# A bank of their own for the transposed chunks of P, three banks for the scores, earlier loads of the network and a new order at the end

## The chip, the cores and the metric

The kernel runs on one core of one Trainium2 chip. The metric is the device time of one execution in microseconds (us). Three runs of the kernel before took 769.55, 768.00 and 767.49 us; their median is 768.0. One further execution was taken with the hardware profiler: 767.24 us, with a span of 765.5 us from the first to the last recorded instruction.

A core has a matrix engine (TensorE, PE in the profile; PEld is its loading of weights), three engines for elementwise work (VectorE or DVE, ScalarE or ACT, GpSimd or POOL) and a queue that issues transfers (SyncE or SP). Each engine works through its own list of instructions in order, and waits at semaphores for the others. TensorE writes its results to PSUM, which has eight banks of 128 x 512 float32; a bank can be given to the next product once its contents have been read out.

## The reference

One transformer layer on `x` (2 x 512 x 512, float32):

```python
q = (hidden_states @ Wq)   # 32 heads of 128
k = (hidden_states @ Wk)   # 8 heads of 128, each for 4 heads of q
v = (hidden_states @ Wv)
scores = jnp.einsum('bhqd,bhkd->bhqk', q, k) * scale   # causal mask, softmax
out = jnp.einsum('bhqk,bhkd->bhqd', probs, v)          # then @ Wo
x = _layernorm(x + attention)
# network: base product and bias, plus eight low-rank experts (rank 16),
# weighted by a sparsemax over eight logits
x = _layernorm(x + base_out + expert_out)
```

## The kernel before, in words

**Precision.** Every operand is split into a high and a low half in float16. A product is three matmuls, high by high, high by low and low by high (`mm3`, L228 to L231). All matmuls of projections, scores, P times V and output therefore have the line L231, and are told apart by their tiles.

**Groups and units.** The work of attention is 16 groups (g, b): a head of K and V with its four heads of Q, for one of two batches. The order of the groups is in L739. A group has four units i = 0 to 3. A unit has 128 rows of scores for each of four steps j (four heads times 32 queries), over n = 128 i + 32 (j + 1) keys. For each unit the kernel has these pieces:

- `proj` (L350): the next group's projections. Unit 0 carries K and the first head of Q, unit 1 the second head, unit 2 V, unit 3 the last two heads. Each is 12 matmuls of 512 columns (tiles pk, pq, pvp) in a bank of tag "pj", evacuated by ScalarE (L235) and VectorE (L236).
- `unit_a` (L362): four scores s, each three matmuls. VectorE masks and takes the row's extreme (L420), ScalarE takes the exponential in place in PSUM (L425), and in pairs `cut_p` forms the reciprocal (L376, L378), the high half (ScalarE, L388) and the low half (VectorE, L391) of P in SBUF, tile phl. Only then is the score's bank free.
- `unit_t` (L438): P is transposed in chunks of up to eight blocks of 128 x 128 on TensorE (`turn_blocks`, L342, tile px). Chunks are copied to SBUF (tile pt) alternately by ScalarE (L345) and VectorE (L348).
- `unit_b` (L450): P times V, tile pv, in the bank "PV", evacuated to o.
- `unit_c` (L491): the output product, 12 matmuls of 512 columns, tile pw, in the bank "wo"; VectorE adds it to the accumulator acc (L504).

**PSUM.** The eight banks are two of tag "pj", four of tag "S" (scores), one "PV" and one "wo". The chunks px share the two "pj" banks with the projections.

**The order.** Within a step of the body, the scores of unit s stand beside the chunks and P times V of unit s - 1, the output product of unit s - 2 and the next group's projections. The order on each engine is made by a list scheduler from the pieces, its own costs and the room in SBUF and PSUM: an instruction whose bank is not yet free in its reckoning comes later in the list. The start (L784 to L875) and the end (`tail`, L930, with the tokens of `TAIL`, L923) are written by hand. In a token the letter is the piece and the digit the block of 128 rows (0 to 7; the last group has 4 to 7): n and N are the layernorm of attention's output, a, p and q the scores and the two cuts of the last group's units, t and b, o their chunks and P times V, c, d their output product, capital letters T, B, O, C, D the same for the group before, X, l, r, s, h, m, e the network's steps, f and F its layernorm and store.

**Preparation.** `plan` and `at` (L881 to L911) attach the loading, measuring and splitting of later weights to units: a generator is advanced at the units that are named. `behind_all` (L887) issues a step no earlier than given instructions. `ffn_setup` (L509) prepares the network: four loads of the base weights (braw), two of the expert's first factor (lraw), one of the second (lorab), one of the bias, then sums of squares on ScalarE (L527) after an addition to the diagonal on GpSimd (L531), scales, and splits. In the kernel before, braw takes the room "base1", and lraw and lorab take three of the six rooms of tag "raw" in which the attention's weights land. `late_x(1, ...)` is the second conversion of x for batch 1.

Of the kernel before, what the change touches and what calls it, by code (L numbers as in the profile page):

```python
# [8 lines left out]
F32 = mybir.dt.float32  # L9
F32R = mybir.dt.float32r  # L10
F16 = mybir.dt.float16
# [6 lines left out]
P = 128  # L18
# [22 lines left out]
def kernel(  # L41
# [58 lines left out]
    def sync_load(dst, src):  # L100
        return nc.sync.dma_start(dst, src)
# [23 lines left out]

    def total(sq, n, name, tag="pj"):

        tot = ps.tile([P, 8], F32, tag=tag, name=f"tot{name}", bufs=4 if tag == "S" else 2)
        nc.tensor.matmul(tot[:, :n], ones, sq[:, :n], start=True, stop=True)
        return tot  # L130

# [96 lines left out]
    def mm3(dst, pairs, first=True, last=True):  # L228
        n = len(pairs)
        for j, (a, b) in enumerate(pairs):  # L230
            nc.tensor.matmul(dst, a, b, start=first and j == 0, stop=last and j == n - 1)  # L231

    def cut_psum(hi, lo, psrc, by):

        nc.scalar.activation(hi, psrc, AF.Copy, scale=by)  # L235
# [32 lines left out]
        LM[(g, b)] = lm  # L268

    def pj(name, tag="pj"):  # L270
        return ps.tile([P, S], F32, tag=tag, name=name, bufs={"pj": 2, "S": 4}.get(tag, 1))

    def mul_k(g, b, tag="pj"):
        pk = pj(f"pk{g}_{b}", tag)
# [62 lines left out]
    def turn_blocks(dst, src, tag="pj"):  # L337

        n = dst.shape[1]
        px = ps.tile([P, 8, P], F16, tag=tag, name="px", bufs=4 if tag == "S" else 2)  # L340
        for k in range(n):
            nc.tensor.transpose(px[:, k, :], src[:, k * P : (k + 1) * P], ident16)  # L342
        count.append(n)
        if len(count) % 2:
            nc.scalar.copy(dst, px[:, :n, :])  # L345
        else:

            nc.vector.tensor_scalar(dst.bitcast(I32), px[:, :n, :].bitcast(I32), 0, None, ALU.bitwise_or)  # L348
# [13 lines left out]
    def unit_a(g, b, i, whole=True):  # L362
# [52 lines left out]
        for j in range(4):  # L415
            n = full + (j + 1) * R
            qh, ql = (q2[:, a, HPG * i + j].rearrange("p h q -> p (h q)") for a in range(2))
            sc = ps.tile([P, S], F32, tag="S", name=f"s{g}_{b}_{i}_{j}", bufs=4)
            mm3(sc[:, :n], [(qh, k2[:, 0, :n]), (qh, k2[:, 1, :n]), (ql, k2[:, 0, :n])])
            nc.vector.tensor_tensor_reduce(  # L420
                out=sc[:, :n], in0=sc[:, :n], in1=mask[:, S - n :], scale=lm[:, 0:1], scalar=BIG,
                op0=ALU.add, op1=ALU.min, accum_out=st[:, 0, j : j + 1],
            )

            nc.scalar.activation(  # L425
                sc[:, :n], sc[:, :n], AF.Exp, bias=st[:, 0, j : j + 1], scale=-1.0, accum_out=st[:, 1, j : j + 1]
            )
            es.append(sc)
            if whole and j % 2:
                cut_p(j - 1)  # L430
# [4 lines left out]
                cut_p(h)  # L435
                yield

    def unit_t(g, b, i, tag="pj"):  # L438

        phl = PH.pop((g, b, i))  # L440
        nb = 8 * i + 6
        PT[(g, b, i)] = pt = sb.tile([P, nb, P], F16, tag="PT", name=f"pt{g}_{b}_{i}", bufs=2)
        for k in range(0, nb, 8):
            n = min(nb, k + 8)
            turn_blocks(pt[:, k:n, :], phl[:, k * P : n * P], tag)
            yield
# [3 lines left out]
    def unit_b(g, b, i):  # L450
# [27 lines left out]
        mm3(dst[:, 2:], pairs)  # L478
        yield
        o2 = sb.tile([P, 2, HPG, 4, R], F16, tag="O", name=f"o{g}_{b}_{i}", bufs=2)  # L480
        cut_psum(o2[:, 0], o2[:, 1], pv, 2.0**-15)
        OT[(g, b, i)] = o2
        yield

# [24 lines left out]
    def ffn_setup():  # L509


        raw = sb.tile([P, KC, HID], F32, tag="base1", name="braw")
        for c in range(KC):
            sync_load(raw[:, c, :], w_base[:, c, :])
        half = KC // 2
        lars = [sb.tile([P, 512], F32, tag="raw", name=f"lraw{k}", bufs=6)[:, : half * NL] for k in range(2)]
        for k, lar in enumerate(lars):
            sync_load(lar.rearrange("p (c n) -> p c n", c=half), lar_in[:, k * half : (k + 1) * half, :])
        lraw = load_raw(lora_b, "lorab")
        bias = sb.tile([P, HID + NE], F32, tag="ffnbias", name="ffnbias")  # L520
        sync_load(bias, bias_in.broadcast_to([P, HID + NE]))
        sq = sb.tile([P, KC, 4], F32, tag="fsq", name="fsq")
# [101 lines left out]
    def turn(t, urgent=False):  # L624
        a = acc[t]
        X[t] = x2 = sb.tile([P, 2 * KC, P], F16, tag="raw", name=f"x2{t}", bufs=6)
        px = ps.tile([P, KC, P], F32, tag="S" if urgent else "pj", name=f"px{t}", bufs=4 if urgent else 2)
        for c in range(KC):
            nc.tensor.transpose(px[:, c, :], a[:, c * P : (c + 1) * P], ident)
        H[t] = px  # L630
        nc.scalar.copy(x2[:, :KC, :], px)
# [13 lines left out]
        mm3(PA[t], pairs, last=False)  # L645

    def lora_in(t, last):
        tag, bufs = ("S", 4) if last else ("pj", 2)
# [28 lines left out]
        H[t] = hw  # L677

    def lora_mid(t, last):
        tag, bufs = ("S", 4) if last else ("pj", 2) if t == NT - 1 else ("wo", 1)  # L680
# [99 lines left out]
    def w_squares(dst, raw, tag):  # L780
        junk = pj("junk", tag)
        nc.scalar.activation(junk, raw, AF.Square, accum_out=dst)

    with tc.manual_schedule(engines={ET.PE, ET.DVE, ET.Activation, ET.Pool, ET.SP}):  # L784
# [40 lines left out]
        w_max(5)  # L825
        amax(mx[:, 6:7], mx[:, 9:13])
        for j in range(4):
            w_squares(sq0[:, j : j + 1], w_raw[j], "S")
        nc.scalar.activation(sq0[:, 4:7], mx[:, 4:7], AF.Square)
        w_lo(5, nc.vector)  # L830
        tot = total(sq0, 7, "0", "S")
# [15 lines left out]
            x_lo(1, c, nc.gpsimd)  # L847
        park(3, "S")
        for k in range(2):
            w_squares(mx[:, 17 + k : 18 + k], wo_raw[k], "S")  # L850
        for c in range(KC):
            x_max(1, c)
        amax(mx[:, 7:8], mx[:, 13:17])
        end_q(0, 0, 2, PK[2])
        end_v(0, 0, PK[5])
        for k in (2, 3):
            w_squares(mx[:, 17 + k : 18 + k], wo_raw[k], "S")
# [42 lines left out]
    at(prepare(0, ROWS, wo_raw), 0, 0, 0)  # L900
    at(prepare(1, JS, w1_raw), 1, 1, 1, 1, 2, 2, 2, 3, 3)
    at(prepare(1, ROWS), 4, 5, 5, 5, 6, 6, 7, 7)
    at(late_x(1, (1, 3)), 5, 6, 7, 7)
    at(ffn_setup(), 20, 21, 21, 21, 21, 21, 28, 28, 29, 29, 36)
    for g in range(1, NG):
        u = NT * (starts[g] - 2) - (3 if g == NG - 2 else 0)
        if g > 1:
# [13 lines left out]


    TAIL = """  # L923
    n3 a7 T7 C6 T7 N3 T7 D6 T7 B7 p7 q7 O7 X3 l3 a6 t7 C7 t7 r3 s3 t7 D7 t7 p6 q6 b7 h3 t6 o7 t6
    m3 t6 a5 c7 b6 p5 q5 e3 d7 t5 o6 n7 t5 a4 c6 N7 p4 q4 b5 f3 X7 t4 l7 m7 o5 r7 d6 n6 s7 c5 N6
    d5 h7 X6 n5 l6 b4 e7 o4 f7 r6 c4 N5 F7 s6 F3 X5 l5 d4 n4 m6 h6 r5 m5 s5 N4 e6 f6 h5 X4 l4 F6
    e5 r4 s4 f5 m4 h4 F5 e4 f4 F4
    """

    def tail():  # L930
# [116 lines left out]
```

## Time and profile before

| what | value |
|---|---|
| median of three runs | 768.0 us |
| profiled execution | 767.24 us |
| its span | 765.5 us |
| TensorE busy | 734.4 us |
| VectorE busy | 570.5 us |
| ScalarE busy | 443.7 us |
| GpSimd busy | 314.0 us |
| DMA, mean share of 16 engines, 100 to 650 us | 0.10 |
| granted clock, mean | 0.99 |

The profile is read by engine first. "Busy" counts the time of recorded instructions. The table of waits names the instruction that waited and the one that released it, with total, number and longest in us. A timeline row gives start and length in us, engine, line, operation, tiles, and in brackets the idle time before it with its releaser. A window row gives its bounds and length, then the busy time and number of instructions on TensorE, weight loads, VectorE, ScalarE and GpSimd, then the granted clock as a share of full speed, the DMA share and GB/s.

### The profile page before, as it was taken

How to read it: one execution, taken by the hardware profiler on the slowest of the kernel's cores; microseconds unless marked ns; L12 is line 12 of the kernel's file. 1: busy time of each engine (PE TensorE's matmuls, PEld its weight loads, DVE VectorE, ACT ScalarE, POOL GpSimd, SP SyncE). 2: the span in 40 equal slices, each digit the busy share in tenths (PEclk: the TensorE clock that was granted, in tenths of full speed). 3: DMA queues.
4: the chain of work that ended last, by engine and by line, in shares of the span. 5: the costliest groups of instructions: out<-in, count | busy, mean ns of one | idle time of the engine just before them, and what ended most of it. 6: DMA issues, size and time to landing. Idle time of an engine off the chain costs nothing.

```text
span 765.5 us, 15512 instructions
## 1 busy us (share of the span) xinstructions
PE 734.4 (96%) x5630; PEld 464.9 (61%) x5630; DVE 570.5 (75%) x1782; ACT 443.7 (58%) x1213; POOL 314.0 (41%) x500
## 2 busy tenths in 40 slices
PE   9899999999998999999999999999999999998896
PEld 6665666566664755666575655666575665655553
DVE  6885877769585777859686796959686687866787
ACT  6795564657466465746556475646556565345520
POOL 5779350726137198544209067243615020200011
PEclk9899999999999999999999999999999999999999
DMA  8540210110102011020202022020000000000001
GB/s 326 211 138 28 57 56 2 48 37 17 41 3 69 2 43 56 28 57 2 55 2 83 1 56 83 2 56 2 1 1 3 1 1 1 15 15 15 1 15 57
DMA packets 17357, 32.21 MB, mean 42 GB/s; under 512 B 1920, under 2 KB 2176, under 8 KB 17280
## 3 DMA queue, kind: packets, MB, share of 16 engines
q1 hardware_dynamic: 17280, 31.22, 13.0%
q8 instruction: 44, 0.72, 0.4%
q14 instruction: 33, 0.27, 0.1%
HBM read 29.12 MB, written 2.10 MB: 41 GB/s over the span
## 4 chain that ended last, share of the span: by engine, by line
PE 54%; DVE 16%; ACT 16%; issue 3%; POOL 2%; DMA 0%; POOLq 0%; ACTq 0%; DVEq 0%
PE pq L231 14%; PE pw L231 12%; PE pv L231 10%; PE s L231 7%; ACT phl L388 6%; ACT s L425 5%; PE px L342 5%; PE pvp L231 3%; DVE phl L391 3%; ACT pt L345 3%; DVE s L420 2%; DVE pt L348 2%; DVE mx L124 2%; PE pa L231 2%; DVE o L236 1%
## 5 line engine op out<-in xcount | busy, mean ns | idle before, releaser
L231 PE MATMUL pw<-w,o 128*128 128x512 f16 x768 | 185.3, 381 | 0.0
L231 PE MATMUL pq<-xT,w 128*128 128x512 f16 x672 | 154.1, 379 | 8.4 <-DVE pt L348 5.2
L391 DVE SCALAR_TENSOR_TENSOR phl<-s,ast,phl 128x128 f16<-128x128 f32 (+7 forms) x352 | 125.7, 418 | 32.8 <-ACT phl L388 30.9
L425 ACT ACTIVATE s<-s,ast 128x320 f32<-128x320 f32 (+15 forms) x256 | 118.5, 464 | 45.8 <-DVE ast L420 32.5
L420 DVE CUSTOM_DVE_ANT_0 s<-s,mask,lm 128x320 f32<-128x320 f32 (+15 forms) x256 | 118.0, 503 | 35.3 <-PE s L231 27.8
L231 PEld LDWEIGHTS <-w 128*128 128x128 f16 x840 | 80.5, 98 | 102.2 <-issue 16.6
L327 POOL TENSOR_SCALAR vt<-vt 64x512 f16<-64x512 f16 (+1 forms) x96 | 58.4, 610 | 164.1 <-ACT vt L235 158.4
L388 ACT ACTIVATE phl<-s,ast 128x96 f16<-128x96 f32 (+11 forms) x304 | 117.5, 478 | 14.1 <-DVE ast L378 13.0
L231 PEld LDWEIGHTS <-o 128*128 128x128 f16 x768 | 72.5, 100 | 69.8 <-issue 1.4
L231 PE MATMUL s<-k,q 128*128 128x480 f16 (+15 forms) x768 | 105.4, 281 | 6.3 <-ACT q L235 3.3
L231 PE MATMUL pv<-pt,vt 128*128 128x256 f16 (+1 forms) x960 | 107.9, 262 | 1.6 <-ACT pt L345 1.5
L231 PEld LDWEIGHTS <-vt 128*128 128x128 f16 x960 | 86.3, 98 | 23.6 <-issue 3.7
L342 PEld LDWEIGHTS <-phl 128*128 128x128 f16 x1152 | 77.5, 98 | 32.4 <-issue 6.4
L342 PE MATMUL px<-ident,phl 128*128 128x128 f16 x1152 | 92.3, 220 | 3.0 <-ACT pt L345 1.5
L345 ACT COPY pt<-px 128x1024 f16<-128x1024 f16 (+1 forms) x80 | 75.3, 941 | 25.2 <-PE px L342 25.2
L235 ACT ACTIVATE o<-pv 128x512 f16<-128x512 f32 x64 | 38.3, 598 | 85.8 <-PE pv L231 85.7
L235 ACT ACTIVATE q<-pq 128x512 f16<-128x512 f32 x56 | 34.4, 615 | 81.4 <-PE pq L231 81.4
L348 DVE TENSOR_SCALAR pt<-px 128x512 int32<-128x512 int32 (+1 forms) x80 | 50.2, 627 | 40.9 <-PE px L342 40.9
L231 PEld LDWEIGHTS <-q 128*128 128x128 f16 x768 | 62.3, 99 | 29.1 <-ACT q L235 4.0
L121 POOL TENSOR_TENSOR w<-raw,w 128x512 f16<-128x512 f32 x70 | 79.5, 1157 | 0.1
L236 DVE SCALAR_TENSOR_TENSOR q<-pq,q 128x512 f16<-128x512 f32 x56 | 38.3, 685 | 40.1 <-ACT q L235 40.0
L263 POOL TENSOR_SCALAR lm<-sc,xs 128x1 f32<-128x1 f32 x15 | 4.0, 264 | 124.5 <-DVE acc L504 124.4
(177 smaller groups left out, 911.4 us busy)
## 6 DMA issues: line engine op xcount, KB each, us to landing
raw<-in_wo_dram SPq DMA_DIRECT2D x32, 256.0 KB, 2.7
raw<-in_wq_dram SPq DMA_DIRECT2D x29, 256.0 KB, 2.8
xraw<-in_xt_dram SPq DMA_DIRECT2D x8, 256.0 KB, 4.8
raw<-in_wk_dram SPq DMA_DIRECT2D x8, 256.0 KB, 2.6
raw_x<-in_xt_dram SPq DMA_DIRECT2D x8, 256.0 KB, 4.2
acc<-in_x_dram SPq DMA_DIRECT2D x8, 256.0 KB, 5.4
out_dram<-y SPq DMA_DIRECT2D x8, 256.0 KB, 2.0
raw<-in_wv_dram SPq DMA_DIRECT2D x7, 256.0 KB, 2.9
```

The lines of the kernel that those rows point to most:

```text
L121: return first.ins, nc.gpsimd.tensor_tensor(lo, view, hi, ALU.subtract).ins
L231: nc.tensor.matmul(dst, a, b, start=first and j == 0, stop=last and j == n - 1)
L235: nc.scalar.activation(hi, psrc, AF.Copy, scale=by)
L236: return nc.vector.scalar_tensor_tensor(lo, psrc, by, hi, ALU.mult, ALU.subtract).ins
L327: nc.gpsimd.tensor_scalar(dst, src, 1.0, 1.0, ALU.mult, ALU.mult)
L342: nc.tensor.transpose(px[:, k, :], src[:, k * P : (k + 1) * P], ident16)
L345: nc.scalar.copy(dst, px[:, :n, :])
L348: nc.vector.tensor_scalar(dst.bitcast(I32), px[:, :n, :].bitcast(I32), 0, None, ALU.bitwise_or)
L388: nc.scalar.activation(dst, src, AF.Copy, scale=by)
L391: nc.vector.scalar_tensor_tensor(dst, src[:, at : at + k], by, p[:, at : at + k], ALU.mult, ALU.subtract)
L420: nc.vector.tensor_tensor_reduce(out=sc[:, :n], in0=sc[:, :n], in1=mask[:, S - n :], scale=lm[:, 0:1], scalar=BIG, op0=ALU.add, op1=ALU.mi ...
L425: nc.scalar.activation(sc[:, :n], sc[:, :n], AF.Exp, bias=st[:, 0, j : j + 1], scale=-1.0, accum_out=st[:, 1, j : j + 1])
```

## The change

1. PSUM is divided anew: the scores have three banks (tag "S") instead of four, the chunks px of the body have one bank of their own (new tag "T") instead of sharing the two of "pj". In the last group, whose units are cut later, the fourth score also uses "T", and the chunks of the last unit of the group before use "pj". Sums of squares at the start write their junk to "T".
2. The network's loads go into x's rooms ("xr1" for braw, "xr0" for lraw and lorab in one tile), which are free once batch 1 of group 0 is projected, in place of "base1" and three "raw" rooms. The steps of `ffn_setup` start at unit 11 instead of 20, and no earlier than the evacuation of P times V of unit (1, 0, 0), for which `cut_psum` now keeps its ScalarE instruction.
3. The second conversion of x for batch 1 follows unit (0, 0, 3) instead of a preparation of weights.
4. `TAIL` has a new order. All four chunks of the unit before (T7) and the cuts p7, q7 precede its P times V (B7), and pieces towards the end change places.

The number of instructions on each engine is the same; the list scheduler lays the body out anew, since the banks are others.

```diff
     def total(sq, n, name, tag="pj"):
-        tot = ps.tile([P, 8], F32, tag=tag, name=f"tot{name}", bufs=4 if tag == "S" else 2)
+        tot = ps.tile([P, 8], F32, tag=tag, name=f"tot{name}", bufs=3 if tag == "S" else 2)
...
+    cut_high = []
+
     def cut_psum(hi, lo, psrc, by):
-        nc.scalar.activation(hi, psrc, AF.Copy, scale=by)
+        cut_high[:] = [nc.scalar.activation(hi, psrc, AF.Copy, scale=by).ins]
         return nc.vector.scalar_tensor_tensor(lo, psrc, by, hi, ALU.mult, ALU.subtract).ins
...
     def turn_blocks(dst, src, tag="pj"):
-        px = ps.tile([P, 8, P], F16, tag=tag, name="px", bufs=4 if tag == "S" else 2)
+        px = ps.tile([P, 8, P], F16, tag=tag, name="px", bufs={"S": 3, "pj": 2}.get(tag, 1))
...
-            sc = ps.tile([P, S], F32, tag="S", name=f"s{g}_{b}_{i}_{j}", bufs=4)
+            tag, n_s = ("S", 3) if whole or j < 3 else ("T", 1)
+            sc = ps.tile([P, S], F32, tag=tag, name=f"s{g}_{b}_{i}_{j}", bufs=n_s)
...
-    def unit_t(g, b, i, tag="pj"):
+    def unit_t(g, b, i, tag="T"):
...
-        cut_psum(o2[:, 0], o2[:, 1], pv, 2.0**-15)
+        lo = cut_psum(o2[:, 0], o2[:, 1], pv, 2.0**-15)
+        LAST[(g, b, i)] = (cut_high[0], lo)
...
     def ffn_setup():
-        raw = sb.tile([P, KC, HID], F32, tag="base1", name="braw")
+        raw = sb.tile([P, KC, HID], F32, tag="xr1", name="braw")
         for c in range(KC):
             sync_load(raw[:, c, :], w_base[:, c, :])
+            if c % 2:
+                yield
         half = KC // 2
-        lars = [sb.tile([P, 512], F32, tag="raw", name=f"lraw{k}", bufs=6)[:, : half * NL] for k in range(2)]
+        rest = sb.tile([P, 3, 512], F32, tag="xr0", name="lraw")
+        lars = [rest[:, k, : half * NL] for k in range(2)]
...
-        lraw = load_raw(lora_b, "lorab")
+        lraw = rest[:, 2, :]
+        sync_load(lraw, lora_b)
...
-            w_squares(sq0[:, j : j + 1], w_raw[j], "S")
+            w_squares(sq0[:, j : j + 1], w_raw[j], "T")
...
-    at(late_x(1, (1, 3)), 5, 6, 7, 7)
-    at(ffn_setup(), 20, 21, 21, 21, 21, 21, 28, 28, 29, 29, 36)
+    at(late_x(1, (0, 0, 3)), 5, 6, 7, 7)
+    def late_ffn():
+        yield from behind_all(ffn_setup(), *LAST[1, 0, 0])
+
+    at(late_ffn(), 11, 12, 13, 21, 21, 21, 21, 21, 28, 28, 29, 29, 36)
...
     TAIL = """
-    n3 a7 T7 C6 T7 N3 T7 D6 T7 B7 p7 q7 O7 X3 l3 a6 t7 C7 t7 r3 s3 t7 D7 t7 p6 q6 b7 h3 t6 o7 t6
-    m3 t6 a5 c7 b6 p5 q5 e3 d7 t5 o6 n7 t5 a4 c6 N7 p4 q4 b5 f3 X7 t4 l7 m7 o5 r7 d6 n6 s7 c5 N6
-    d5 h7 X6 n5 l6 b4 e7 o4 f7 r6 c4 N5 F7 s6 F3 X5 l5 d4 n4 m6 h6 r5 m5 s5 N4 e6 f6 h5 X4 l4 F6
-    e5 r4 s4 f5 m4 h4 F5 e4 f4 F4
+    T7 n3 a7 T7 p7 N3 T7 C6 T7 q7 B7 O7 D6 t7 t7 X3 l3 t7 C7 t7 a6 r3 s3 p6 b7 D7 q6 h3 m3 o7 t6
+    t6 t6 a5 p5 q5 c7 b6 d7 t5 o6 t5 n7 e3 a4 p4 N7 q4 c6 b5 X7 f3 l7 t4 o5 m7 d6 r7 n6 s7 c5 N6
+    d5 h7 X6 l6 b4 e7 r6 o4 c4 f7 n5 F7 N5 X5 F3 s6 d4 l5 m6 n4 r5 s5 N4 h6 m5 e6 f6 h5 X4 l4 e5
+    F6 r4 s4 f5 m4 h4 e4 f4 F5 F4
     """
...
-        T6 = {first + NT - 1: unit_t(*groups[-2], NT - 1)}
+        T6 = {first + NT - 1: unit_t(*groups[-2], NT - 1, "pj")}
```

The remaining lines of the diff replace four banks by three wherever the tag "S" is named (`pj`, `turn`, `lora_in`, `lora_mid`), and "S" by "T" in the other sums of squares.

More of the change, by code (lines that the diff above doesn't have):

```diff
@@ L270, in pj @@
     def pj(name, tag="pj"):
-        return ps.tile([P, S], F32, tag=tag, name=name, bufs={"pj": 2, "S": 4}.get(tag, 1))
+        return ps.tile([P, S], F32, tag=tag, name=name, bufs={"pj": 2, "S": 3}.get(tag, 1))
     def mul_k(g, b, tag="pj"):
@@ L626, in turn @@
         X[t] = x2 = sb.tile([P, 2 * KC, P], F16, tag="raw", name=f"x2{t}", bufs=6)
-        px = ps.tile([P, KC, P], F32, tag="S" if urgent else "pj", name=f"px{t}", bufs=4 if urgent else 2)
+        px = ps.tile([P, KC, P], F32, tag="S" if urgent else "pj", name=f"px{t}", bufs=3 if urgent else 2)
         for c in range(KC):
@@ L647, in lora_in @@
     def lora_in(t, last):
-        tag, bufs = ("S", 4) if last else ("pj", 2)
+        tag, bufs = ("S", 3) if last else ("pj", 2)
         lar, x2 = F["lar"], X[t]
@@ L679, in lora_mid @@
     def lora_mid(t, last):
-        tag, bufs = ("S", 4) if last else ("pj", 2) if t == NT - 1 else ("wo", 1)
+        tag, bufs = ("S", 3) if last else ("pj", 2) if t == NT - 1 else ("wo", 1)
         ph = ps.tile([P, P], F32, tag=tag, name=f"phw{t}", bufs=bufs)
@@ L849 @@
         for k in range(2):
-            w_squares(mx[:, 17 + k : 18 + k], wo_raw[k], "S")
+            w_squares(mx[:, 17 + k : 18 + k], wo_raw[k], "T")
         for c in range(KC):
@@ L856 @@
         for k in (2, 3):
-            w_squares(mx[:, 17 + k : 18 + k], wo_raw[k], "S")
+            w_squares(mx[:, 17 + k : 18 + k], wo_raw[k], "T")
         amax(sq1[:, 1:2], mx[:, 17:21])
```

## The prediction

> **What bounds the kernel now.** I read the totals of the page first, then the table of waits of TensorE, then the busy time by stage, then the timeline where a wait is long.
>
> ```profile
> PE 734.4 (96%) x5630; PEld 464.9 (61%) x5630; DVE 570.5 (75%) x1782; ACT 443.7 (58%) x1213; POOL 314.0 (41%) x500
> PEclk9899999999999999999999999999999999999999
> ```
>
> TensorE is busy for 96% of the span. Busy is not yet streaming. In back-to-back rows a 512-column matmul starts 0.216 us after the one before it. If every matmul took its columns at that pace, the stretch from first to last matmul (758 us) would need 701 us, so some 57 us are waits, slow-clock stretches and small gaps. By start-to-start gaps they lie so: 12.3 us before 45 us, 4.6 from 45 to 100, 24.5 from 100 to 650, 0.9 from 650 to 690, 15 from 690 to the end. A change of order or of buffers can only move these 57 us; no instruction is added or taken away on any engine.
>
> ```profile
> 100.00:650.00 550.00, 539.42 (x4288) 339.22 (x4286) 410.01 (x1271) 327.74 (x911) 234.66 (x367) 1.00 0.10 28
> 687.10:720.20 33.10, 27.70 (x223) 18.06 (x221) 22.39 (x74) 18.03 (x42) 1.09 (x2) 0.95 0.02 9
> 725.90:759.70 33.80, 31.70 (x208) 17.13 (x205) 30.16 (x112) 7.79 (x24) 4.55 (x8) 1.00 0.07 25
> ```
>
> Columns: window, length, busy time of TensorE, its weight loads, VectorE, ScalarE, GpSimd, granted clock, DMA share, GB/s. The long middle is TensorE's and runs at clock 1.00. The stage from 687 loses most, 5.4 of 33.1 us not busy and a clock of 0.95. The last 34 us are VectorE's as much (30.16 of 33.80).
>
> ```profile
> PE pq L231 <- DVE pt L348: 5.2, 12, 0.7
> PE s L231 <- ACT q L235: 3.3, 2, 1.7
> PE pq L231 <- ACT pt L345: 2.7, 9, 0.4
> PE px L342 <- ACT pt L345: 1.5, 2, 1.1
> PE pv L231 <- ACT pt L345: 1.5, 1, 1.5
> PE s L231 <- DVE phl L391: 1.2, 1, 1.2
> ```
>
> Columns: total, times, longest. First and third are one thing: a projection (pq) waits for a pj bank that holds transposed chunks (px) not yet copied out, 21 times, 7.9 us. The scores wait hardly ever for their four banks (the last row, once).
>
> **The main loop.** One group of four units is a period of about 42.9 us, 41.7 of it streaming; 13 lie between 100 and 650 us.
>
> ```profile
> 291.31 0.68 DVE L348 TENSOR_SCALAR pt<-px 128x512 int32<-128x512 int32 x1
> 292.04 0.38 PE L231 MATMUL pq<-xT,w 128*128 128x512 f16 x1 [0.41 <-DVE pt L348]
> 286.45 0.62 PE L231 MATMUL s<-k,q 128*128 128x32 f16 x12
> 289.40 0.49 DVE L391 SCALAR_TENSOR_TENSOR phl<-s,ast,phl 128x32 f16<-128x32 f32 x2 [0.86 <-ACT phl L388]
> ```
>
> *Taken away.* Chunks no longer use pj banks, so the pq waits go. In the period from 286.45 they stretch start-to-start by 0.57 (the wait at 292.04) and 0.51 (at 323.7); with a score's wait of 0.10, 1.18 us go. In the next period waits of 1.41 stand.
>
> *Added: the fourth score.* With three banks it waits until the first score's bank is free, and it is moved behind other matmuls; behind it in TensorE's strict order stand the rest of pk, the other projections, pw and pv, and VectorE's and ScalarE's softmax of that unit. In unit 0 the first score starts at 286.45 and its last reader ends near 289.65 (first of the two at 289.40), 3.2 us on. The fourth now comes after nine score matmuls (0.35), eight transposes (0.42) and ten of pk (10 x 0.216), 2.9 us on: wait 0.30. Walking the other units alike, with each softmax step at its row's duration: unit 1 0.15, unit 2 0.25 for its second score (its bank is that of the unit before) and 0.15 for its fourth, unit 3 0.20 and 0.30.
>
> *Added: one bank for all chunks.* The next chunk waits for the copy of the last. From 294.63 to the end of ScalarE's copy (296.33) 1.25 us pass after the last transpose; five pw matmuls (1.08) lie between the two chunks: 0.23 once per period. Elsewhere a projection of 12 (2.59) covers it. If pw stood elsewhere, the whole 1.25 would show.
>
> Sum of that period: 0.30 + 0.23 + 0.15 + 0.25 + 0.15 + 0.20 + 0.30 = 1.58 against 1.18, +0.40. The next, walked alike: 1.93 against 1.41, +0.52. Mean +0.46, times 13: **+6.0 us**. Bounds: if nothing new waits, -1.3 x 13 = -17. If banks come free as late as they do before, where nobody hurries (first score to release 3.07 in unit 0, 4.5 to 4.8 in unit 1, 5.6 to 5.9 in unit 2, 6.5 in unit 3, against distances of 2.9, 3.6 to 4.2, 3.8 to 5.4 and 5.4 to 6.4), the new waits reach 3.5 a period, +2.2 net, +29. I take the walk, since it uses rows of the same operations in the new order; it lies nearer the lower end, and its error is one-sided: a queue I took as free can only delay.
>
> The Trainium skill, Perfetto Trace Analysis, section Optimizing Tensor Performance, says that independent matmul groups should rotate through different PSUM banks so that one's evacuation lies beside the next one's matmuls, and it reads regular bubbles as a sign of too few buffers. One bank for chunks and three for scores go against it; the row at 292.04 agrees on the bubble. By that rule alone each of a period's ten chunks but one would bare what is not covered, and the main loop would end near its upper bound.
>
> **The network's loads.** The four base loads, lraw and lorab move ahead on SP, behind x's last loads and before the second group's later weights, about 60 to 75 us by SP's order now; the squares (L527) move on ScalarE to about 95 to 110 us. Before:
>
> ```profile
> 238.73 0.63 ACT L527 ACTIVATE warm<-raw_lorab 128x512 bf16<-128x512 f32 x1 [3.68 <-DMA raw_lorab<-in_lora_b_dram]
> 240.75 0.22 PE L231 MATMUL s<-k,q 128*128 128x32 f16 x2 [1.60 <-ACT q L235]
> 243.05 3.14 PE L231 MATMUL pk<-xT,w 128*128 128x512 f16 x10
> 54.25 0.78 ACT L345 COPY pt<-px 128x768 f16<-128x768 f16 x1
> 55.08 0.82 PE L231 MATMUL pv<-pt,vt 128*128 128x256 f16 x6 [1.46 <-ACT pt L345]
> ```
>
> ScalarE stands 3.68 us for one load, q's evacuation is queued behind it, the scores wait 1.60 and 0.51, and the matmuls after run at half pace (the ten of pk: four at 0.43 instead of 0.216). Together 3.25 us go: **-3.3**. What is late next there is the period's ordinary waits. Bounds: 0 (a load still late at its new place; the queue then has the same wait) and -3.3. At 54.25 the copy is queued behind four squares that wait for GpSimd's add, which waits for a load; 1.5 of pv's wait goes. Against that the loop's new waits (one period, about +0.5) begin: **-1.0**, bounds -1.5 and +1.5, the latter if SP's seven loads (the 256 KB loads land in 2.6 to 5.4 us) delay weights of group 2. These have their use over 20 us later; that is the cover. With x's second conversion earlier (late_x), GpSimd and ScalarE do the same work in another order in 45 to 100 us; they are busy 36.8 and 36.1 of 55, so I cost that at nothing. The clock of 0.92 before 45 us has its cause before any moved instruction and stays.
>
> The Trainium skill, TensorE: Matmul & The Clock Gate, Part 1, has the clock fall to half after an idle window of about 3.4 us. The row at 243.05 shows half pace after two waits of 2.1 us in all; a window that needs full idleness would not have tripped, so by that rule only 2.1 us would be regained.
>
> **The end.** From the last group's first score (687.07) to its last (end 720.15) TensorE takes 33.1 us for 23.6 of streaming.
>
> ```profile
> 697.50 0.63 PE L629 MATMUL px<-ident,acc 128*128 128x128 f32 x4 [0.62 <-DVE phl L391]
> 699.88 1.27 PE L231 MATMUL s<-k,q 128*128 128x320 f16 x6 [1.22 <-DVE phl L391]
> 703.21 3.88 PE L231 MATMUL pw<-w,o 128*128 128x512 f16 x12
> ```
>
> The 9.5 of excess are 0.57 and 0.79 at transposes and pv up to 697, 1.38, 0.25 and 0.75 at scores, 1.05 of half clock at 703, 1.26, 0.50, 0.73 and 0.44 at chunks after, and small gaps. In the new order p7 and q7 (the softmax's cuts) come ahead of B7 and all four T7 chunks ahead of it too, so the scores' banks come free while TensorE has pv. Walking it: pv waits 1.4 for the last T7 copy, chunks of t7 wait 0.9 and 1.5 on theirs, the last unit's scores 1.1 and 0.6: 5.5, so 29.1 us: -4.0, and -0.3 for half clock less. **-4.3**; bounds -9.5 (no wait left) and +1.5 (mine doubled). From 725.9 VectorE sets the pace with the same instructions, so the shift carries to the end; the swapped last pieces give **-0.1** (0 to -0.5). The store of y after the last row (759.7 to 765.5) stays. The stage 650 to 687 has 0.9 of excess: nothing to gain, a score's wait of up to 1 to lose; taken as 0.
>
> Sum: +6.0 - 3.3 - 1.0 - 4.3 - 0.1 = -2.7. The profiled execution took 767.24 us (765.5 of span and 1.7 around), so 764.5; the median of the runs is 768.0, 0.8 above, and carried to it 765.3. I state 765.0.
>
> **Rivals.** *R1, slower: the score banks.* Place: the fourth score in units 1 to 3. Its bank is released by VectorE's low parts (418 ns mean, L391), which queue behind copies of chunks (627) and weight maxima (0.64 each) on an engine busy 410 of 550 us. One such operation in front of a release at two more places per period adds some 0.8 a period, 10 us: 775. It decides from +0.42 a period over my walk (5.4 / 13, to 770.4). For it: the old latencies exceed the new distances in all units. Against: the list of instructions places the fourth where the bank is expected. The Trainium skill's rule on rotating banks (the same page and section) points to this case; no row of before shows three banks, so it keeps the chance that the old latencies give it. *R2: the waits cancel.* Half the tail's gain is eaten (-2) and the loop costs +0.5 a period: +0.1, about 767.5. *R3: hardly any new wait* (fourth score and copies on time): +6.0 becomes -10, 749 to 757. For it: VectorE and ScalarE have 25% and 42% idle. Against: the walk finds waits at seven places. *R4: the edit of the loads does nothing,* a load being late at another place: +3.3, 768.
>
> **Chances.** Forecast (761 to 765.7) 0.37, R3 0.08, R2 and R4 0.20, R1 0.35. About 0.3% (2.3 us) is what a measurement of this kernel can tell from no change. So faster 0.45, same 0.20, slower 0.35. The range must reach into R1, which is open upward, and below into R3: 757 to 777; the forecast's own is 761 to 769.
>
> **What would show it.** Right: the pairs of pq and pt vanish from TensorE's waits; s waits for phl (L391) and px for pt (L345, L348) appear, 10 to 60 times with 0.1 to 0.4 each; 100 to 650 us of old work take 4 to 8 us more; no ScalarE wait on raw_lorab; 687 to 720 shorter by 3 to 5. Wrong: s waits over 20 us in all (R1), or TensorE busy in the loop as now (R3).

## The result and the profile after

The changed kernel took 756.0 us (median of four runs, 755.46 to 756.80), the kernel before beside it 768.3 (767.49 to 769.55): a ratio of 0.9838, 95% interval 0.9823 to 0.9854. Measured again on another chip it was 756.2 against 768.1, 0.9846 (0.9831 to 0.9860). So the change saves 12 us. I had forecast 765.0 with 757 to 777 around it. The sign was right. The gain is four times what I forecast, and the time lies below my range.

The page's totals of the changed kernel, and its clock in 40 slices:

```profile
PE 734.1 (97%) x5630; PEld 458.8 (61%) x5630; DVE 578.8 (77%) x1782; ACT 449.6 (60%) x1213; POOL 313.8 (42%) x500
PEclk9999999999999999999999999999999999999998
```

TensorE is busy as long as before (734) in a span of 755.0 us instead of 765.5; by these records what went is its idle time. The second slice's clock was 8 tenths before and is 9 or more now. TensorE's longest waits now are these (total, times, longest):

```profile
PE s L231 <- DVE phl L393: 1.7, 5, 0.6
PE wps L73 <- DVE warm L70: 1.2, 1, 1.2
PE px L638 <- DVE acc L627: 1.1, 2, 0.9
PE s L231 <- ACT pt L347: 0.9, 2, 0.5
PE s L231 <- ACT q L237: 0.8, 1, 0.8
```

The 21 waits of a projection for a chunk's copy are gone, as forecast. The waits of scores for phl that I expected "10 to 60 times" are in this table 5 times, 1.7 us. The table holds idle time after the recorded end of the matmul before, so it misses the short ones: the waits of the main loop are read from starts, below. The profiled executions were 767.24 and 756.80 us. To see where the 10.4 between them went, take the start of the first matmul of a group's first score (a timeline row such as the one at 286.45) in both kernels:

| first score of group | before | changed | difference |
|---|---|---|---|
| (0,1), second group | 67.07 | 62.82 | -4.26 |
| (1,0) | 110.32 | 105.86 | -4.47 |
| (2,0) | 196.07 | 192.29 | -3.78 |
| (3,0) | 286.45 | 279.02 | -7.43 |
| (7,1), last group | 687.07 | 681.78 | -5.28 |
| last matmul's end | 759.78 | 748.91 | -10.87 |

So the start gives 4.5 us, 110 to 196 costs 0.7, 196 to 286 gives 3.65 (the stall at 239), the loop from 286 to 687 costs 2.15, the end gives 5.6. After the last matmul 0.4 us are lost again. The loop, as one window each, before first:

```profile
286.45:687.07 400.62, 394.22 (x3139) 247.61 (x3136) 301.77 (x943) 232.29 (x643) 157.96 (x239) 1.00 0.09 25
```

```profile
279.02:681.78 402.76, 397.78 (x3146) 246.72 (x3144) 308.71 (x948) 235.75 (x644) 159.57 (x243) 1.00 0.09 25
```

### The profile page after: what moved, and what is told of

It is laid out like the page before. It is cut to its first block, busy times and chain, and to the rows that moved or that the text cites. A ratio compares the mean times of both kernels' runs of the same rounds, so it can differ in the third digit from the quotient of the medians.

```text
span 755.0 us, 15509 instructions
## 1 busy us (share of the span) xinstructions
PE 734.1 (97%) x5630; PEld 458.8 (61%) x5630; DVE 578.8 (77%) x1782; ACT 449.6 (60%) x1213; POOL 313.8 (42%) x500
## 4 chain that ended last, share of the span: by engine, by line
PE 56%; ACT 12%; DVE 12%; issue 2%; ACTq 0%; DVEq 0%
PE pw L231 14%; PE pq L231 13%; PE pv L231 9%; PE s L231 9%; PE px L344 5%; ACT s L428 4%; PE pvp L231 3%; ACT pt L347 3%; DVE phl L393 3%; ACT phl L390 3%; DVE s L423 2%; PE pa L231 2%; ACT o L237 1%; ACT q L237 1%; PE pk L231 1%
## 5 line engine op out<-in xcount | busy, mean ns | idle before, releaser
L393 DVE SCALAR_TENSOR_TENSOR phl<-s,ast,phl 128x128 f16<-128x128 f32 (+7 forms) x352 | 128.8, 418 | 39.2 <-ACT phl L390 39.0
L231 PE MATMUL pq<-xT,w 128*128 128x512 f16 x672 | 158.5, 379 | 0.0
L423 DVE CUSTOM_DVE_ANT_0 s<-s,mask,lm 128x320 f32<-128x320 f32 (+15 forms) x256 | 121.5, 505 | 43.0 <-PE s L231 41.2
L390 ACT ACTIVATE phl<-s,ast 128x96 f16<-128x96 f32 (+11 forms) x304 | 121.7, 465 | 27.6 <-DVE ast L380 26.6
L231 PE MATMUL s<-k,q 128*128 128x480 f16 (+15 forms) x768 | 116.7, 279 | 7.3 <-DVE phl L393 1.7
L329 POOL TENSOR_SCALAR vt<-vt 32x512 f16<-32x512 f16 (+1 forms) x96 | 58.2, 610 | 127.3 <-ACT vt L237 121.8
L231 PE MATMUL pv<-pt,vt 128*128 128x256 f16 (+1 forms) x960 | 105.3, 262 | 0.2 <-DVE pt L350 0.2
L344 PE MATMUL px<-ident,phl 128*128 128x128 f16 x1152 | 95.9, 219 | 2.4 <-ACT phl L390 0.6
L508 DVE SCALAR_TENSOR_TENSOR acc<-pw,lm,acc 128x512 f32<-128x512 f32 x64 | 47.8, 747 | 13.5 <-PE pw L231 13.4
L118 POOL TENSOR_SCALAR raw<-raw,sc 128x512 f32<-128x512 f32 x70 | 47.8, 692 | 11.2 <-issue 5.2
```

The costliest lines, as they stand in the source:

```text
L118: nc.gpsimd.tensor_scalar(view, view, by, 1.0, ALU.mult, ALU.mult)
L329: nc.gpsimd.tensor_scalar(dst, src, 1.0, 1.0, ALU.mult, ALU.mult)
L390: nc.scalar.activation(dst, src, AF.Copy, scale=by)
L393: nc.vector.scalar_tensor_tensor(dst, src[:, at : at + k], by, p[:, at : at + k], ALU.mult, ALU.subtract)
L423: nc.vector.tensor_tensor_reduce(out=sc[:, :n], in0=sc[:, :n], in1=mask[:, S - n :], scale=lm[:, 0:1], scalar=BIG, op0=ALU.add, op1=ALU.mi ...
```

## The experiments

In the tables "start" is the difference to the kernel before at the first score of group (0,1), and so on; all from the profiled execution of each kernel.

**One part alone.** First, the order of the end on the old banks.

```diff
-    n3 a7 T7 C6 T7 N3 T7 D6 T7 B7 p7 q7 O7 X3 l3 a6 ...
+    T7 n3 a7 T7 p7 N3 T7 C6 T7 q7 B7 O7 D6 t7 t7 X3 ...
```

> The kernel before with nothing changed but the new TAIL order (four score banks, chunks in the pj banks). Theory A, the order itself frees the score banks in time: the stretch from the last group's first score to its last falls by 4 to 6 us and the time by the same, to about 763 (ratio 0.992 to 0.995). Rival B, the gain at the end needs the new banks (the chunks of the unit before and the fourth score no longer beside each other in pj and S): -2 to +1 us.

Measured 762.8 against 766.8, ratio 0.9953 (0.9936 to 0.9970). From the last group's first score on it is 5.3 us faster. Theory A holds: the order itself gains, without any new bank. TensorE, ScalarE and VectorE have the same instructions in the same order as before up to about 687 us, and yet the second group's first score comes 1.7 us later than in the kernel before, and 1.0 of it is made up at the stall at 239. So much do two profiles of one order differ.

Second, the loads of the network alone.

```diff
-        raw = sb.tile([P, KC, HID], F32, tag="base1", name="braw")
+        raw = sb.tile([P, KC, HID], F32, tag="xr1", name="braw")
...
-    at(ffn_setup(), 20, 21, 21, 21, 21, 21, 28, 28, 29, 29, 36)
+    at(late_ffn(), 11, 12, 13, 21, 21, 21, 21, 21, 28, 28, 29, 29, 36)
```

> The kernel before with the network's loads alone in x's rooms and issued early; banks and TAIL as before. Theory A: the stall at 239 us goes (about -3.9 us by the two traces) and pv's wait at 53 us (-1.5), together -5 to -6, about 763. Rival B: the start gains from the loads all of what separates the two traces there (-4.4), together -8. Rival C: only the stall at 239 us goes, -3.5.

Measured 760.2 against 766.8, 0.9922 (0.9901 to 0.9942). The start gains 2.6 us, 196 to 286 gains 3.4. That is theory A by the time. Of the 2.6, however, 1.4 are there when the third unit's first score starts (40.02 instead of 41.37), where TensorE, ScalarE and VectorE still have the same instructions in both kernels; so the loads give about 1.2 of it, by the wait of pv (1.46 before, 0.28 here). And 110 to 196 costs 0.7, the stretch in which the squares now stand.

Third, the banks alone.

```diff
-            sc = ps.tile([P, S], F32, tag="S", name=f"s{g}_{b}_{i}_{j}", bufs=4)
+            tag, n_s = ("S", 3) if whole or j < 3 else ("T", 1)
...
-    def unit_t(g, b, i, tag="pj"):
+    def unit_t(g, b, i, tag="T"):
```

> The kernel before with the new banks alone (three for scores, one for chunks, the start's sums of squares in the chunks' bank; the TAIL order, the loads and x's conversion as before). Theory A: the start gains about 2 us since the sums of squares no longer take score banks, each period of the loop costs 0.2 us more (+2.5 us), the end changes by less than 1: 0 +- 1.5 us. Rival B, my prediction's term: +6 in the loop, so +4 to +6 us in all. Rival C: the loop costs nothing and the start gains, -2 us.

Measured 777.6 against 766.8, 1.0158 (1.0131 to 1.0184): 11 us slower, worse than every theory. But the loop is not where it lost them: from 286 to 687 it costs 1.7 us. The start costs 5.6, the stall at 239 stays, and two waits of TensorE at the start stand out, of 6.0 and 3.0 us. Of TensorE's and ScalarE's timeline at the first:

```profile
43.62 0.29 PE L342 MATMUL px<-ident,phl 128*128 128x128 f16 x1 [6.01 <-ACT phl L388]
```

```profile
42.16 0.72 ACT L117 ACTIVATE xT<-raw_x,sc 128x512 f16<-128x512 f32 x1 [5.89 <-DMA raw_x<-in_xt_dram]
42.79 0.40 ACT L426 ACTIVATE s<-s,ast 128x224 f32<-128x224 f32 x1
43.12 0.19 ACT L426 ACTIVATION_READ_ACCUMULATOR s<-s,ast 128x1 f32 x1
43.21 0.90 ACT L388 ACTIVATE phl<-s,ast 128x128 f16<-128x128 f32 x3
```

With the new banks the scheduler lays x's second conversion (L117) ahead of the second unit's exponentials. There it waits 5.89 us for its load, and the exponential, P's high half and TensorE's chunk are queued behind it.

Fourth, the changed kernel with the start's sums of squares back in a score bank.

```diff
-            w_squares(sq0[:, j : j + 1], w_raw[j], "T")
+            w_squares(sq0[:, j : j + 1], w_raw[j], "S")
```

> The changed kernel with the start's eight sums of squares written to a score bank again. Theory A, these squares held the first scores up: first scores about 1 us later, the two waits behind them (1.07 and 0.43 in the kernel before) back, +2 to +2.6 us, about 758.3. Rival B, the start gains from another part (loads, x's conversion): within 0.5 us of 756.

Measured 757.4, 0.9885 (0.9865 to 0.9906) of before. The first score comes 0.80 us later than before instead of 0.28 earlier, as theory A says, but by group (0,1) the start is 4.7 us ahead, no less than in the changed kernel. The delay of the first score is made up. Theory A falls for the start as a whole; the time itself lies between the two theories (758.3 and 756).

**The changed kernel less one part.** Four kernels, each undoing one part. First the banks: four for scores, the chunks in "pj", the start's sums in "S".

```diff
-            tag, n_s = ("S", 3) if whole or j < 3 else ("T", 1)
+            sc = ps.tile([P, S], F32, tag="S", name=f"s{g}_{b}_{i}_{j}", bufs=4)
...
-    def unit_t(g, b, i, tag="T"):
+    def unit_t(g, b, i, tag="pj"):
```

> The changed kernel with four score banks and the chunks in the pj banks again: the kernel before plus the network's loads, x's later conversion and the new TAIL. Theory D, the gain is that of those three and the new banks only cost in the loop (0.2 us a period): 1.5 to 3 us faster than the changed kernel, 13 to 15 us faster than before (ratio 0.980 to 0.983). Rival E, the banks are what makes the start and the end fast: 2 us or more slower than the changed kernel, ratio 0.987 or more.

Then x's later conversion.

```diff
-    at(late_x(1, (0, 0, 3)), 5, 6, 7, 7)
+    at(late_x(1, (1, 3)), 5, 6, 7, 7)
```

> The changed kernel with x's second conversion tied to the earlier instruction again. Theory D: the four conversions stand on ScalarE ahead of the second unit's exponentials and wait for their loads (5.9 us in the run with the banks alone), P's chunks wait behind them: 5 to 7 us slower than the changed kernel, ratio to before 0.991 to 0.995. Rival F: the wait of that run came from the network's loads in the raw rooms, which here are elsewhere: within 1 us of the changed kernel.

Then the loads (with the rooms of before).

```diff
-    at(late_ffn(), 11, 12, 13, 21, 21, 21, 21, 21, 28, 28, 29, 29, 36)
+    at(ffn_setup(), 20, 21, 21, 21, 21, 21, 28, 28, 29, 29, 36)
```

> The changed kernel with the network's loads at their old place and in the old rooms. Theory D: the wait for lorab near 235 us comes back (3.5 us) and that for braw near 50 us (3 us as in the run with the banks alone): 6 to 7 us slower than the changed kernel, ratio to before 0.992 to 0.994. Rival: the wait near 50 us belonged to x's conversion, 3.5 us slower, 0.989.

Then the order of the end.

```diff
-    T7 n3 a7 T7 p7 N3 T7 C6 T7 q7 B7 O7 D6 t7 t7 X3 ...
+    n3 a7 T7 C6 T7 N3 T7 D6 T7 B7 p7 q7 O7 X3 l3 a6 ...
```

> The changed kernel with the TAIL order of before. Theory D: 5 to 7 us slower than the changed kernel (the banks alone lost 1.7 at the end against before, the new order gained 5.3 on the old banks), ratio to before 0.992 to 0.994. Rival G, on three banks the old order costs no more than on four: 4 us slower, 0.989.

| kernel | us | ratio to before (interval) | start | 286 | 687 | end |
|---|---|---|---|---|---|---|
| changed | 756.0 | 0.9838 (0.9823 to 0.9854) | -4.3 | -7.4 | -5.3 | -10.9 |
| less the banks | 756.6 | 0.9855 (0.9837 to 0.9874) | -2.4 | -4.5 | -4.2 | -9.6 |
| less x's later conversion | 764.6 | 0.9966 (0.9953 to 0.9979) | +4.2 | +1.1 | +3.0 | -2.3 |
| less the loads | 773.5 | 1.0080 (1.0064 to 1.0096) | +8.2 | +9.3 | +11.4 | +5.9 |
| less the new end | 761.2 | 0.9920 (0.9906 to 0.9934) | -4.4 | -7.5 | -5.8 | -5.1 |

Less the banks, neither theory held: the time is about that of the changed kernel. The banks' gain at the start (1.9 us) and their cost in the loop nearly cancel. Less x's later conversion loses 8.4 us, all at the start; theory D's mechanism, with a size above its 5 to 7. The wait in its table is the one of the kernel with the banks alone:

```profile
ACT xT L117 <- DMA raw_x<-in_xt_dram: 9.1, 2, 5.7
```

Less the loads loses 17 us, not 6 to 7. Again it is the start, 12.4 us of it; the rest is the stall at 239, which is back. TensorE's and all engines' waits:

```profile
PE px L344 <- ACT v L237: 10.0, 1, 10.0
```

```profile
ACT warm L531 <- POOL braw L535: 11.5, 1, 11.5
POOL braw L535 <- DMA braw<-in_base_dram: 6.4, 4, 5.3
```

With x's conversion moved away, the network's squares stand next on ScalarE, and ScalarE waits 11.5 us for one of them while v's evacuation is queued behind. Less the new end loses 5.7 us by the last matmul, 6.2 of it after the last group's first score (and 0.5 gained ahead of it); on the new banks the old order is 0.65 us slower there than on the old ones. Theory D.

**Side by side, and a version between.** The changed kernel, the four-bank one again, and two kernels with the new banks for the first two or four groups only.

```diff
-            tag, n_s = ("S", 3) if whole or j < 3 else ("T", 1)
+            tag, n_s = ("S", 3) if j < 3 or whole and groups.index((g, b)) < 4 else ("T", 1)
...
-    def unit_t(g, b, i, tag="T"):
+    def unit_t(g, b, i, tag=None):
+        tag = tag or ("T" if groups.index((g, b)) < 4 else "pj")
```

> The changed kernel itself, beside the next three on one chip. By the first result 0.9838 of before (0.982 to 0.985), some 12 us.

> The changed kernel with the old banks, again, beside it on one chip. By the two traces the new banks gain 1.9 us before 67 us, cost 2.1 us between 286 and 687 and the rest is within 1: so this is 1 to 1.5 us slower than the changed kernel. Rival: the loop's cost decides and the start's gain is chance, 1 to 2 us faster.

> New banks for the first two groups alone; from the third on the fourth score takes the chunks' bank (as in the last group of the changed kernel) and the chunks the two pj banks, which is four banks for scores again. Theory H, start and loop are separate: the start's gain stays and the loop costs nothing, 1.5 to 2.5 us faster than the changed kernel. Rival I, a fixed bank for the fourth score and three that rotate make it wait beside the old pq waits: equal to the changed kernel or up to 2 us slower.

> The same with the new banks for the first four groups. Theory H: 1.2 to 2 us faster than the changed kernel (two periods more at 0.2 us), the stall of lorab gone as in it. Rival I: equal or up to 2 us slower.

| kernel | us | ratio to before (interval) | start | 286 | 687 | end |
|---|---|---|---|---|---|---|
| changed again | 756.2 | 0.9846 (0.9831 to 0.9860) | -5.5 | -8.6 | -6.5 | -11.1 |
| four banks again | 756.8 | 0.9850 (0.9834 to 0.9867) | -2.8 | -5.0 | -4.7 | -10.1 |
| new banks, two groups | 756.0 | 0.9846 (0.9832 to 0.9861) | -5.4 | -7.4 | -7.1 | -10.8 |
| new banks, four groups | 755.3 | 0.9835 (0.9821 to 0.9850) | -4.6 | -7.6 | -6.8 | -11.8 |

The loop of the two first, as windows (changed, then four banks):

```profile
277.82:680.54 402.72, 397.76 (x3147) 246.73 (x3144) 308.51 (x948) 235.76 (x644) 159.61 (x243) 1.00 0.09 25
```

```profile
281.48:682.34 400.86, 394.65 (x3147) 248.02 (x3145) 302.04 (x944) 232.50 (x644) 157.94 (x239) 1.00 0.09 25
```

The banks cost the loop 402.72 - 400.86 = 1.9 us, on one chip, and the second profile of each repeats the first to 0.1 us. In the time of the whole, the changed kernel is 0.6 us ahead of the four-bank one, less than the 1 to 1.5 expected, and the intervals overlap: the banks are not shown to gain anything. From 286 to 687 the mixed kernels lose only 0.4 and 0.8 us against before, so fourth score and chunks in their old share of banks cost little again: theory H for the loop. Its times did not come: 0.3 and 0.9 us faster than the changed kernel, where it had 1.5 to 2.5 and 1.2 to 2. With two groups, 1.1 us less than in the changed kernel beside it is gained between 67 and 286, and 0.9 less at the end. The median of the four-group kernel is 0.9 us under the changed one; the intervals overlap, so it is not shown to be faster.

**What the start gains from the banks.** One more kernel has the mixed banks from the first group on, so chunks never have their own bank.

```diff
-            tag, n_s = ("S", 3) if whole or j < 3 else ("T", 1)
+            tag, n_s = ("S", 3) if j < 3 else ("T", 1)
...
-    def unit_t(g, b, i, tag="T"):
+    def unit_t(g, b, i, tag="pj"):
```

> The changed kernel with the fourth score in the chunks' bank and the chunks in the pj banks for all groups, the first two included; the start's sums of squares keep a bank that is not a score's of the first three. Theory J, the start's further gain (2 us before 67 us against the four-bank kernel) is from the chunks' own bank: the first score of the second group comes 2.3 to 3 us earlier than before, not 4.3 to 5.4, and the time is 757 to 758. Theory K, it is from the score bank that the sums of squares leave alone: 4.3 to 5.4 us earlier, 755 to 756.

Measured 756.2 against 766.9, 0.9864 (0.9848 to 0.9881); start -4.9. The chunks' own bank is not the main part of what gains there: theory J falls, the start is in K's range, while the time is at K's edge. But K's own reason is contradicted by the fourth experiment, where the squares are in a score bank and the start is as fast. What the fast starts share is seen first in TensorE's rows at the first scores. First the four-bank kernel, then this one, then the changed kernel in its first profile:

```profile
25.39 0.25 PE L231 MATMUL s<-k,q 128*128 128x32 f16 x3 [1.47 <-ACT q L237]
26.55 0.38 PE L129 MATMUL tot<-sq,ones 128*128 128x2 f32 x2 [0.91 <-DVE sq L124]
28.07 2.16 PE L231 MATMUL pk<-xr,wr 128*128 128x512 f32 x5 [0.29 <-DVE sc L138]
```

```profile
24.46 0.40 PE L231 MATMUL s<-k,q 128*128 128x32 f16 x6 [0.78 <-ACT q L237]
24.81 0.38 PE L129 MATMUL tot<-sq,ones 128*128 128x2 f32 x2
26.20 3.04 PE L231 MATMUL pk<-xr,wr 128*128 128x512 f32 x12 [0.29 <-DVE sc L138]
```

```profile
24.74 0.28 PE L231 MATMUL s<-k,q 128*128 128x32 f16 x4 [0.78 <-ACT q L237]
25.16 0.38 PE L129 MATMUL tot<-sq,ones 128*128 128x2 f32 x2
26.55 3.83 PE L231 MATMUL pk<-xr,wr 128*128 128x512 f32 x9 [0.35 <-DVE sc L138]
```

In the four-bank kernel two waits of 1.47 and 0.91 lie a microsecond apart, and five of pk take 2.16 us, about half pace. Here there is one wait of 0.78, and twelve take 3.04. In the fourth experiment, too, there was one wait (1.82, ahead of tot) and twelve in 3.02. So with the banks laid out anew the scheduler's first rows differ, one of two waits goes or shrinks, and pk starts some 1 to 2 us earlier. The slow-clock stretch behind it goes only sometimes: of the eight profiles whose TensorE has the changed kernel's first rows, three have it (the changed kernel, less the new end, new banks for four groups) and five don't; the five profiles on the old banks all have it. To see the whole start, take from each matmul's start to the next, and subtract 0.216 us per 512 columns. What is left, in us:

| kernel | granted clock, 24 to 40 us | 22 to 36 us | 36 to 45 | 45 to 56 | 56 to second group | sum |
|---|---|---|---|---|---|---|
| before | 0.79 | 7.0 | 0.9 | 2.3 | 1.0 | 11.2 |
| end's order alone | 0.79 | 6.7 | 0.9 | 2.9 | 2.1 | 12.5 |
| loads alone | 0.89 | 5.7 | 0.9 | 1.2 | 0.7 | 8.6 |
| four banks again | 0.89 | 5.7 | 0.9 | 0.9 | 0.8 | 8.4 |
| changed | 0.89 | 4.5 | 0.7 | 0.9 | 0.2 | 6.3 |
| changed again | 1.00 | 3.3 | 1.4 | 0.8 | 0.1 | 5.6 |
| fourth score in the chunks' bank, all groups | 1.00 | 3.4 | 1.2 | 0.7 | 0.8 | 6.0 |

(Before 22 us the profiles differ by up to 0.6 us, so the sums do not give the starts exactly.) From 45 to 56 it is the loads' gain. From 56 on it is the chunks' own bank: 0.6 to 0.7 us, among them a projection's wait for a chunk's copy (0.24 of idle time with four banks again, 0.18 in the last row's kernel, none in the changed one). From 22 to 36 the changed kernel gains 1.2 us on four banks at the same granted clock, and another 1.2 where the clock stays full, of which 0.7 is gone again by 45 us. Which change of banks brings the first rows' order about stays open; the three rotating score banks are in all of the kernels that have such rows, and were not tried alone.

## Why the prediction was wrong, point by point

The measured change is -12.3 us by medians and -10.4 by the profiled executions; up to the last matmul's end it is -10.9, where I had -2.7. The rest of the gap to the medians is the spread of runs: the profiled one of the changed kernel was its slowest of four, and that of the kernel before was faster than any of the four beside it. In the terms of the forecast, with the four-bank kernel as the line between loop and loads:

| term | forecast | measured | second profile |
|---|---|---|---|
| the start, to the third group | -1.0 | -4.5 | -5.7 |
| the loop's new waits less the old, 110 to 687 | +6.0 | +1.6 | +1.7 |
| the rest of 110 to 687 (the loads) | -3.3 | -2.4 | -2.5 |
| the end | -4.4 | -5.6 | -4.6 |
| sum | -2.7 | -10.9 | -11.1 |

Two steps failed: the loop's new waits were priced 4.4 us too high, and the start was missing the first rows and had a sign wrong, 3.5 us. The other two terms together are off by 0.3.

*The start, -1.0, measured -4.3 (-5.5 in the second profile) at the second group.* I had -1.5 for pv's wait at 53 us, and 45 to 56 us gave 1.3 (1.5): right. I had +0.5 for new waits of the loop; none is seen, and 0.8 to 0.9 of old ones went, from 56 us on. And I wrote that the slow clock before 45 us "has its cause before any moved instruction and stays": 22 to 36 us gave 2.5 (3.7). The first scores are moved instructions, and it went in part. Some of that is not the change's, since 1.3 of it are seen with the loads alone, in the same rows at another clock.

The other failure cost the forecast nothing, by luck. I wrote of x's second conversion that it comes earlier, the same work in another order, "so I cost that at nothing", with ScalarE busy 36.1 of 55 us as the cover. It comes later: at 76 to 82 us instead of 43 to 51. And the cover is an average. ScalarE works in order, and one conversion that waits for its load holds up everything behind it: with the new banks and the old tie it costs 8.4 us. With four banks the later tie gains nothing (start -2.4 with it, -2.6 without, in the two kernels with the loads moved). So the edit is a guard that the new banks need, and I had not looked for what it guards against. My bound of +1.5 was also far too small for the start of the kernels between: +5.6 with the banks alone and +8.2 less the loads.

*The loop, +6.0, measured +1.6 to +2.6.* The mechanism was right, the size was too large by more than two. Against the four-bank kernel it is +1.9 from 286 to 687, 9.3 periods, 0.20 a period, 2.6 for thirteen. Over all of 110 to 687 it is +1.6. Wait by wait, in the period from 279.02 (start-to-start excess, beside the forecast): unit 0's fourth score 0.31 (0.30), the chunk 0.23 (0.23), unit 1 0.29 (0.15), unit 2 0.06 (0.25 + 0.15), unit 3 0.20 and 0.19 (0.20 and 0.30). Two rows that carry it, of the changed kernel:

```profile
282.23 0.33 PE L231 MATMUL s<-k,q 128*128 128x128 f16 x3
304.90 0.66 PE L231 MATMUL s<-k,q 128*128 128x384 f16 x3
```

The first score of unit 0 started at 279.02, so the fourth came 3.2 us on, as walked. In unit 2 the fourth (304.90) started 0.06 us after its bank came free, and lost almost nothing. There I had charged 0.34 that didn't come, about the whole by which the walk was too high (1.58 against 1.28). The old waits I had read rightly: 1.28 less 1.18 is +0.10, and the period went from 42.93 to 43.03. The next went from 43.17 to 43.40, +0.23 where I had +0.52. So each walk was 0.3 us too high, and a net of two nearly equal sums takes the whole of such an error, thirteen times. I also called the error one-sided upwards; it went the other way.

*The network's loads, -3.3, measured -3.4 to -3.65 from 196 to 286.* Right in place and size. "Earlier loads" holds for lraw and lorab alone, issued at 59 to 60 us instead of 231 to 236. The four base loads come later, at 57 to 59 instead of 23 to 48, and that is what takes their squares, and pv's wait, off the start. The squares came at 127 to 135 us, not 95 to 110, and the kernels on four banks with the loads moved are 0.7 us slower from 110 to 196, which I had left out. The row where scores waited 1.60 now has none:

```profile
235.31 0.45 PE L231 MATMUL s<-k,q 128*128 128x32 f16 x9
236.05 2.32 PE L231 MATMUL pk<-xT,w 128*128 128x512 f16 x10
```

Ten of pk take 2.32 us instead of 3.14. By the Trainium skill's rule (TensorE: Matmul & The Clock Gate, Part 1: the clock falls after at least one idle window of about 3.4 us) only the 2.1 us of waits were to be regained, if that window must be idle throughout. The measurement decides: half pace came after waits of 1.60 and 0.51, and its loss went too. But it is no fixed part of this stall. The kernel with the end's order alone has the same instructions and nearly the same waits here, and pk at full pace:

```profile
242.25 0.21 PE L231 MATMUL s<-k,q 128*128 128x32 f16 x2 [1.43 <-ACT q L235]
243.84 2.75 PE L231 MATMUL pk<-xT,w 128*128 128x512 f16 x12
```

So about 0.8 us of the 3.4 to 3.65 are a slow-clock stretch that one profile of the old order had and the other had not.

*The end, -4.3, measured -5.6 (-4.6 in the second profile).* The mechanism was right: -5.3 by the order alone on the old banks, and the shift carries on to the last matmul. The walk was not: it left 5.5 us of waits (pv 1.4, chunks 0.9 and 1.5, scores 1.1 and 0.6), and by start-to-start gaps the same places have 2.1 (0.40, 0.51 and none, 0.70 and 0.50). Part of this the later steps lose again. I had also taken 720.15 for the end of the last group's scores; it is the third unit's, and the fourth unit's end at 727.3. Half-clock pw did not come back in this profile:

```profile
693.29 2.75 PE L231 MATMUL pw<-w,o 128*128 128x512 f16 x12
706.91 0.37 PE L231 MATMUL s<-k,q 128*128 128x160 f16 x3 [0.54 <-ACT pt L347]
707.61 1.02 PE L231 MATMUL s<-k,q 128*128 128x192 f16 x9 [0.33 <-ACT pt L347]
```

Twelve of pw in 2.75 us where they took 3.88. In the second profile, with the same instructions, the next twelve have it:

```profile
707.58 4.07 PE L231 MATMUL pw<-w,o 128*128 128x512 f16 x12
```

*The rivals.* R1 (score banks the bound, 775) did not come: VectorE is recorded busy 7 us longer inside the loop's window, and releases still come on time. Its price per place was about right in units 0 and 1, and wrong that it adds up. R3's time (749 to 757) came, but not its mechanism: the loop did not gain 10 us, it lost 2. Its time is luck. The Trainium skill (Perfetto Trace Analysis, section Optimizing Tensor Performance) says that independent matmul groups should rotate through banks. The trace agrees in sign, 1.9 us for one bank less to rotate through, and shows how small it is where other matmuls lie in between.

## What to carry to other kernels

Ask of an edit that ties a step to a later point what would stand at the head of an in-order queue without it; a share of busy time does not answer that, since one instruction that waits for a transfer holds up the whole queue. The price of parts that the scheduler lays out together is not the sum of the parts alone (here +11, -7 and -4 for three of them, and -12 for all; x's later conversion was not run alone), so undo each from the whole as well. Undone so, the banks are worth 0.6 us, the new end 5, x's later tie 9 and the loads 17. And one bank less costs little if every wait for it has matmuls to stand behind: walk the wait by start-to-start gaps on both sides before charging it.

## What the runs showed that I had not expected

The same kernel has different clocks in its first microseconds. In the changed kernel's first profile nine of pk took 3.83 us after a wait of 0.78; in its second, after waits of 0.79 and 0.28, twelve took 3.01:

```profile
24.28 0.28 PE L231 MATMUL s<-k,q 128*128 128x32 f16 x4 [0.79 <-ACT q L237]
24.85 0.38 PE L129 MATMUL tot<-sq,ones 128*128 128x2 f32 x2 [0.28 <-DVE sq L124]
26.23 3.01 PE L231 MATMUL pk<-xr,wr 128*128 128x512 f32 x12 [0.35 <-DVE sc L138]
```

The start differs by 1.2 us between the two, mostly for that. The Trainium skill, TensorE: Matmul & The Clock Gate, Part 1, says that the activity window runs freely, so that the point of the change of clock varies. These two profiles agree with it. A difference of one or two microseconds at the start of two kernels is therefore not read from one profile each. Over many runs, though, the changed kernel does have fewer slow stretches: its eight runs have a mean granted clock of 0.995 to 0.999, the seven runs of the kernel before beside the second four 0.987 to 0.993. The eight of the four-bank kernel have 0.995 to 0.999 too, so the banks are not shown to do that.
